# Sums taken from counts, two accumulators for the adj product, and score rows broadcast by transfers

## The chip, the core and the metric

The kernel runs on one core of a Trainium2 chip. The core has a matrix engine (TensorE, PE in the profile; its weight loads appear as PEld), a vector engine (DVE), a scalar engine (ACT), GpSimd (POOL) and a sync engine (SP) that issues most transfers. Each engine takes its instructions in the order in which the program issues them. The metric is device time in microseconds (us): 2310.74 before, the median of three runs (2310.22 to 2312.15).

## The reference, cut to what matters

Two graph layers over N = 3327 nodes of 256 features, with a weighted adjacency `adj` (3327 x 3327). Each layer's input is a layer norm followed by a Relu.

Layer 0 has two steps. Each step builds an attention matrix and keeps, per row, the largest probabilities that add up to 0.9:

```python
logits = q @ k.T                      # (N, N); q, k from Xa
probs = softmax(logits)
keep_sorted = cs - sp < TOP_P         # cs: running sum of sorted probabilities
A = probs * mask; A = A / A.sum(-1)
Xf = R @ Xf                           # R: adj plus identity, rows normalised
Xa = A @ Xa
Z = Z + Xf @ U1[n].T + Xa @ U2[n].T
```

After it come a residual, a layer norm and a second residual. Layer 1 is a four-head neighbour attention:

```python
e = leaky_relu(s[:, :, None] + d[:, None, :], 0.2)
attn = softmax(where(adj > 0, e, -inf), axis=2)
out = elu(einsum('hij,jhf->ihf', attn, hp))
```

## The kernel before, in words

The 3327 nodes are cut into NT = 26 row tiles of P = 128. All work is in `fast`; a second, long form, `general`, runs only if a test at the end of `fast` finds that a row's search failed.

**Order of the work.** The kernel doesn't write its instructions in a loop. Pieces of work are handed to a planner (`Plan.put`), each with its engine, an estimated length, a rank, the pieces it needs and the buffers it takes and gives back (for instance `accf`, `acca`, `px`, `pl`, `et`, `e`, `at`). The planner plays the pieces through with these estimates and issues them in the order that results. On the chip the order on each engine is then fixed.

**A row tile in a step of layer 0** (`search`, `attention`). PE makes the logits (L842), ACT takes their exponentials into a buffer `e` of 128 x 3327 and their sums (L853). A first threshold `t0` is guessed. Then the threshold is refined: the step needs, for the threshold t, how many elements of a row lie below it and what they add up to. Before the change both come from two passes of ACT over the row (`count`, L890): a Sign pass whose sum gives the count, and a Relu pass whose sum gives the sum below. POOL computes the next threshold from them (`step`, L905 to L932). Step 1 of the layer evaluates two thresholds (`EVALS`), so four ACT passes; step 2 evaluates three, the third with a pass of DVE instead (`sum_below`, L936). DVE then lists the candidates near the threshold (`window`, L947 and L952), picks the exact one (`sort`, `choose`) and zeroes the dropped elements in four pieces (`drop`, L1002). PE turns the row's 26 blocks of 128 x 128 (L1015, into `px`), ACT copies them to `et` (L1020, three buffers), and PE multiplies them with the features (L1027, into `acca`).

**The adj product** (`class Full`, `full`). For each row tile, 26 matmuls (L1053) add adj tiles times features into one PSUM accumulator, `accf`; adj comes through four buffers `at` of four tiles each (L1047). ACT copies the finished sum to `f` (L1060), DVE adds it up (L1069). There is one `accf`, so the next row tile's first matmul needs the copy of the last one. These products are PE's reserve: the planner puts them where softmax rows aren't ready.

**Layer 1's weights** (`layer1_weights`). One piece issues four loads (L706 to L709) into `late` and an `et` buffer and at once the DVE products and sums that need them (L713, L719), in another `et` buffer. It stands at the start of step 1, after the last use of the weights that lie in the same memory.

**From layer 0 to layer 1** (`finish2`). Each finished row is normed and projected (L1282, L1291); ACT copies the result and takes exponentials `qd` and `low` (L1296, L1297); DVE keeps the scores in `sd` (L1301).

**Layer 1** (`attend_neighbours`). The output nodes are cut into four blocks of W = 832. For a block, the exponentials of its source scores must stand on all 128 partitions (`both`): `broadcast` has PE transpose a column spread over 128 columns (L1460, four heads for each of seven tiles, into `px`), and ACT takes the exponential (L1464). The target is the memory of `c`, free only when all adj products are done. For each of the 26 neighbour tiles: two adj loads (L1500, 512-byte pieces), a mask on ACT (L1510 Relu, L1511 Sign, into `et`), four DVE operations, one per head (L1522), into one of six buffers (four `e`, two in the memory of `rhs`), then 8 product matmuls (L1538) and 8 matmuls for the sums (L1552, into the PSUM of `acca` and `accf`, three tiles at a time). At a block's end ACT copies the sums out (L1592, L1595), PE turns them (L1613), DVE and ACT finish (L1617, L1625 to L1630).

The functions that the change touches:

Of the kernel before, what the change touches and what calls it, by code (L numbers as in the profile page):

```python
# [19 lines left out]
P = 128  # L20
# [550 lines left out]
def fast(  # L571
# [35 lines left out]
    low = const.tile([P, NT, H], F32, name="low")  # L607

# [17 lines left out]
    with ExitStack() as l0:  # L626
# [73 lines left out]
        def layer1_weights():  # L700
# [8 lines left out]
            nc.sync.dma_start(wa[:, :, : H * FH], gat_w.rearrange("(c p) o -> p c o", p=P))  # L709
            prod = etpool.tile([P, 2, H, FH], F32, name="et")  # L710
# [9 lines left out]
            return g_all, b_all, wa  # L720
# [90 lines left out]
        plan = Plan(dict(pl=2, px=2, acca=1, accf=1, et=3, at=4, y=1, e2=2, mask=2, **BUFS))  # L811

        class Row:
# [3 lines left out]
                "b v w t0 t1 t2 u g k2 p0 p1 p2 p3 j0 j1 j2 j3 r0 s0 B0 B1 B2 q d dt least up h0 h1 room K zs nxt cnt m "  # L817
# [67 lines left out]
            def count(self, k, fn):  # L885

                junk = scr.tile([P, NP], mybir.dt.float8e5, name="junk")
                dst = (self.r0, self.s0)[fn == AF.Sign]
                t = (self.t0, self.t1, self.t2)[k]
                S.activation(junk[:, :N], self.e[:, :N], fn, bias=t, scale=-1.0, accum_out=dst, saturate=False)  # L890

            def step(self, k, eng):

# [10 lines left out]
                if k < 2:  # L904
                    TS(self.q, self.s0, float(N), t, ALU.add, ALU.mult)  # L905
                    TS(B, self.r0, -2.0, self.q, ALU.mult, ALU.add)
                else:
                    TS(B, B, 2.0, None, ALU.mult)
                TS(self.d, B, -0.5, self.b, ALU.mult, ALU.add)
                if k == 0:  # L910

                    TS(self.g, self.u, cs[:, self.i : self.i + 1], 0.25, ALU.mult, ALU.min)
                    TS(self.least, self.s0, N - 2.0 * (WIN[self.n] - 2), BIG, ALU.is_ge, ALU.mult)
                    TS(self.least, self.d, 0.0, self.least, ALU.is_ge, ALU.mult)
                else:
                    TT(self.u, B, (self.B0, self.B1)[k - 1], ALU.subtract)
# [16 lines left out]

            def sum_below(self):
                y = scr.tile([P, NP], BF16, name="y")
                V.scalar_tensor_tensor(  # L936
                    y[:, :N], self.e[:, :N], self.t2, self.e[:, :N], ALU.is_lt, ALU.mult, accum_out=self.B2
                )
# [98 lines left out]
        class Full:  # L1037


            def __init__(self, n, t):  # L1040
                self.n, self.t, self.at = n, t, {}
                self.src, self.w = (main, D + 1) if n == 0 else (c, D)

# [5 lines left out]
            def some(self, js):  # L1049
                for j in js:  # L1050
                    if j == 0:
                        self.acc = ps_a.tile([P, D + 1], F32, name="accf")
                    T.matmul(  # L1053
# [190 lines left out]
        def finish2(row, done, z, rank):  # L1244
# [48 lines left out]
            def stage():  # L1293
# [3 lines left out]
                S.activation(low[:, t, :], f[:, H * FH + H :], AF.Exp, scale=ALPHA - 1.0)  # L1297

# [22 lines left out]
            a = plan.put("ACT", 0.72, r, stage, needs=[a], take=["f"], give=["px", "xt"])  # L1321
            return plan.put("DVE", 0.6, r, scale, needs=[a], give=["f"]), s_
# [20 lines left out]
        def search(row, rank, keys, stats_of, fresh):  # L1343
# [22 lines left out]
            for j in range(2):  # L1366
                got = [plan.put("ACT", 3.05, rank - (2.1, 1.7)[j], row.count, j, fn, needs=[a]) for fn in (AF.Relu, AF.Sign)]
                a = plan.put("POOL", (3.8, 4.7)[j], rank - (2.0, 1.6)[j], row.step, j, GP, needs=[got, more])
            if EVALS[n] == 3:
                a = plan.put("DVE", 3.65, rank - 1.3, row.sum_below, needs=[a], take=["y"], give=["y"], lag=0.02, hold=3.6)  # L1370
# [36 lines left out]
        def full(n, t, rank, right, after):  # L1407
# [7 lines left out]
            for j in range(0, NT, 2):  # L1415
# [3 lines left out]
                    take=["accf"] * (j == 0), give=["at"] * last,  # L1419
                )  # L1420
            a = plan.put("ACT", 0.3, -90.0, f.copy, needs=[a], take=["f"], give=["accf"])
# [5 lines left out]
        def attend_neighbours(rows, ends, done, fulls):  # L1427
# [5 lines left out]
            logits_done = rows[-1].pieces["logits"]  # L1433
# [7 lines left out]
            def open_heads():  # L1441
                extra["both"] = halves_of("c", None)

            def open_more():
                extra["e"] = halves_of("rhs", None)

            opened = plan.put("SP", 0.02, 59.0, open_heads, needs=[fulls], lag=0.0)
            more = plan.put("SP", 0.02, 59.0, open_more, needs=[freed], lag=0.0)

            def broadcast(b, rank):  # L1450

                lo, hi = b * W, (b + 1) * W
                got = []
                for t in range(lo // P, -(-hi // P)):
                    held = {}

                    def turn(t=t, held=held):
                        held["pb"] = ps_x.tile([P, H, P], F32, name="px")
                        for k in range(H):
                            T.transpose(held["pb"][:, k, :], sd[:, 0, t, k : k + 1].to_broadcast([P, P]), ident)  # L1460

                    def exps(t=t, held=held):
                        x0, x1 = max(lo, t * P), min(hi, t * P + P)
                        S.activation(  # L1464
                            extra["both"][b % 2][:, :, x0 - lo : x1 - lo],
                            held["pb"][:, :, x0 - t * P : x1 - t * P],
                            AF.Exp,
                            scale=1.0 - ALPHA,
                        )

                    a = plan.put("PE", 0.55, rank, turn, needs=[ends[t][0], opened, used_heads[b % 2]], take=["px"])
                    got.append(plan.put("ACT", 0.65, rank, exps, needs=[a], give=["px"]))
# [5 lines left out]
            for b in range(4):  # L1478
# [14 lines left out]
                for j in range(NT):  # L1493
                    rank = r0 + 9.0 * j / NT
                    held = {}

                    def load(g, j=j, held=held, tiles=tiles):
# [15 lines left out]
                    def exponents(a, j=j, held=held, b=b):  # L1513
                        if a == 0:
                            k = j % 6
# [250 lines left out]
```

## Time and profile before

| engine | busy us | share of the span | what it mostly does |
|---|---|---|---|
| PE | 2223.0 | 96% | attention L1027 (623.6), adj product L1053 (322.8 and 317.0), layer-1 products L1538 |
| DVE | 1699.8 | 74% | window L947, L952, drop L1002, layer-1 exponents L1522 |
| ACT | 1559.9 | 68% | counts L890 (638.9, 208 of 3.07), copies L1020, exponentials L853 |
| POOL | 1017.6 | 44% | threshold steps L905 to L932 |

The span of the profiled run is 2307.9 us. The stages, from the windows of the trace: the start up to about 120 us; step 1 up to about 980; step 2 to about 1740; the passage to layer 1 to about 1820; layer 1 to about 2280; the end. A PE matmul of fp32 appears as two records, a transpose as one. The records' modelled ends overlap, so a busy PE is not necessarily a PE at its pace: the number of records in a window tells more. A line such as "PE px L1015 <- ACT et L1020" reads: this group of PE sat idle until that ACT group released it.

### The profile page before, as it was taken

What the parts mean: (1) busy time and instruction counts of PE and PEld (TensorE: products, weight loads), DVE (VectorE), ACT (ScalarE), POOL (GpSimd) and SP (SyncE); (2) the same over time, 40 slices, a digit from 0 to 9 for tenths busy, and PEclk for the clock granted to TensorE, in tenths of its full rate; (3) what the DMA queues carried; (4) which work ended last, traced back from release to release, by engine and by line L of the source; (5) the groups of instructions that cost most, each with busy time, mean ns of one, the idle gap of its engine ahead of it and who ended that gap; (6) DMA issues with size and microseconds to landing.
All of it is one profiled execution on the core that took longest, in us unless ns stands there. A gap on an engine that the chain in (4) does not pass through costs nothing. (4 is left out here: it accounts for less than half of the span.)

```text
span 2307.9 us, 36154 instructions
## 1 busy us (share of the span) xinstructions
PE 2223.0 (96%) x11956; PEld 1551.9 (67%) x11956; DVE 1699.8 (74%) x4299; ACT 1559.9 (68%) x2901; POOL 1017.6 (44%) x2263
## 2 busy tenths in 40 slices
PE   7989999999999999999999999999998999999997
PEld 5467777777877778777777778777877434333332
DVE  5564666656645664389889889889888797989895
ACT  5767788678777862488676787777773556565553
POOL 6345455445554541357766765677774000000000
PEclk9999999999999999999999999999999999999998
DMA  3021212212212222522212222122223343434341
GB/s 97 1 68 52 68 54 60 64 53 61 73 47 72 68 87 73 176 85 65 65 51 68 68 76 67 53 62 68 71 67 99 90 114 109 116 99 127 100 130 42
DMA packets 189654, 176.97 MB, mean 77 GB/s; under 512 B 14866, under 2 KB 145808, under 8 KB 189328
## 3 DMA queue, kind: packets, MB, share of 16 engines
q1 hardware_dynamic: 187472, 173.30, 25.8%
q8 instruction: 96, 1.57, 0.3%
q10 hardware_dynamic: 1984, 1.26, 0.2%
q14 instruction: 102, 0.84, 0.1%
HBM read 157.66 MB, written 15.89 MB: 75 GB/s over the span
## 5 line engine op out<-in xcount | busy, mean ns | idle before, releaser
L890 ACT ACTIVATE junk<-e,sc 128x3327 fp8e5<-128x3327 f32 x208 | 638.9, 3072 | 25.4 <-POOL sc L931 23.4
L1027 PE MATMUL acca<-rhs,et 128*128 128x256 f32 x2704 | 623.6, 381 | 2.3 <-ACT et L1020 2.2
L1027 PEld LDWEIGHTS acca<-rhs,et 128*128 128x128 f32 x2704 | 500.6, 191 | 66.9 <-ACT et L1020 4.8
L1053 PE MATMUL accf<-c,at 128*128 128x256 f32 x1352 | 322.8, 388 | 20.4 <-ACT f L1060 20.3
L947 DVE SCALAR_TENSOR_TENSOR y<-e,sc 128x1664 f32<-128x1664 f32 x104 | 204.6, 1967 | 187.0 <-POOL sc L928 169.3
L1053 PE MATMUL accf<-main,at 128*128 128x257 f32 x1352 | 317.0, 383 | 4.8 <-DMA at<-in_adjt_dram 4.5
L1020 ACT COPY et<-px 128x512 f32<-128x512 f32 (+1 forms) x364 | 194.4, 554 | 186.4 <-PE acca L1027 125.3
L1053 PEld LDWEIGHTS accf<-c,at 128*128 128x128 f32 x1352 | 251.6, 192 | 78.4 <-ACT f L1060 28.8
L1522 DVE SCALAR_TENSOR_TENSOR e<-c,low,et 128x832 f32<-128x832 f32 x288 | 289.1, 1075 | 16.8 <-ACT e L1592 9.5
L1053 PEld LDWEIGHTS accf<-main,at 128*128 128x128 f32 x1352 | 250.9, 191 | 46.4 <-issue 8.0
L952 DVE MAX8 cands<-y 128x8 f32<-128x208 f32 x832 | 241.1, 361 | 3.6
L1002 DVE SCALAR_TENSOR_TENSOR e<-e,thr 128x832 f32<-128x832 f32 x208 | 214.0, 1083 | 2.6 <-ACT kq L1178 0.5
L1538 PE MATMUL pl<-e,main 128*64 128x416 f32 x1152 | 212.6, 516 | 0.1
L1015 PE MATMUL px<-ident,e 128*128 128x128 f32 x1352 | 196.4, 277 | 16.8 <-ACT et L1020 7.9
L853 ACT ACTIVATE e<-pl 128x1024 f32<-128x1024 f32 x208 | 179.3, 865 | 45.6 <-PE pl L842 44.7
L1015 PEld LDWEIGHTS px<-ident,e 128*128 128x128 f32 x1352 | 163.4, 143 | 57.5 <-issue 13.6
L1511 ACT ACTIVATE et<-at 128x512 bf16<-128x512 f32 (+1 forms) x208 | 114.5, 550 | 118.3 <-DVE e L1522 76.9
L842 PE MATMUL pl<-kt,qq 64*128 64x512 f32 (+1 forms) x728 | 184.1, 588 | 0.0
L905 POOL TENSOR_SCALAR sc<-sc 128x1 f32<-128x1 f32 x104 | 40.2, 386 | 309.3 <-ACT junk L890 249.3
L1538 PEld LDWEIGHTS pl<-e,main 128*64 128x64 f32 x1152 | 79.6, 137 | 123.1 <-issue 104.0
L936 DVE SCALAR_TENSOR_TENSOR y<-e,sc 128x3327 bf16<-128x3327 f32 x26 | 95.5, 3672 | 47.9 <-POOL sc L931 47.9
L1522 DVE SCALAR_TENSOR_TENSOR rhs<-c,low,et 128x832 f32<-128x832 f32 x128 | 129.2, 1073 | 0.0
(485 smaller groups left out, 3076.8 us busy)
## 6 DMA issues: line engine op xcount, KB each, us to landing
at<-in_adjt_dram SPq DMA_DIRECT2D x416, 256.0 KB, 2.8
at<-in_adjt_dram SPq DMA_DIRECT2D x104, 192.0 KB, 3.0
at<-in_adjt_dram SPq DMA_DIRECT2D x52, 128.0 KB, 2.1
ys<-ystage SPq DMA_DIRECT2D x26, 256.0 KB, 2.4
rhs<-in_x_dram SPq DMA_DIRECT2D x26, 128.0 KB, 3.3
ystage<-in_x_dram SPq DMA_DIRECT2D x26, 128.0 KB, 2.1
base<-ys SPq DMA_DIRECT2D x26, 128.0 KB, 2.2
x1s<-ystage SPq DMA_DIRECT2D x26, 128.0 KB, 1.7
```

Source lines behind the costliest of these rows:

```text
L842: T.matmul(pl[:, r, :m], qq[half, self.i, :], kt[half, 512 * k : 512 * k + m], start=True, stop=True,)
L853: S.activation(self.e[:, 1024 * k : 1024 * k + pl.shape[1]], pl, AF.Exp, accum_out=(self.p0, self.p1, self.p2, self.p3)[k],)
L890: S.activation(junk[:, :N], self.e[:, :N], fn, bias=t, scale=-1.0, accum_out=dst, saturate=False)
L947: V.scalar_tensor_tensor(self.y[:, : hi - lo], self.e[:, lo:hi], self.up, self.e[:, lo:hi], ALU.is_lt, ALU.mult, accum_out=(self.h0, self. ...
L952: V.max(self.cands[:, o // PIECE, :], self.y[:, o - lo : min(o + PIECE, hi) - lo])
L1002: V.scalar_tensor_tensor(piece, piece, self.thr[:, o : o + 1], piece, ALU.is_gt, ALU.mult)
L1015: T.transpose(pt[:, k, :], self.e[:, j * P : (j + 1) * P], ident)
L1020: S.copy(self.et[g][:, :m, :], self.pt.pop(g)[:, :m, :])
L1027: T.matmul(self.acc, et[:, j - 4 * g, :], rhs[self.n][:, j, :], start=(j == 0), stop=(j == NT - 1))
L1053: T.matmul(self.acc[:, : self.w], self.at[j // JC][:, j % JC, :], self.src[:, j, : self.w], start=(j == 0), stop=(j == NT - 1),)
L1522: V.scalar_tensor_tensor(held["e"][:, k, :], extra["both"][b % 2][:, k, :], low[:, j, k : k + 1], held["mask"], ALU.max, ALU.mult,)
L1538: T.matmul(q["acc"][a][k * FH : (k + 1) * FH, c, :C], main[:, j, h * FH : (h + 1) * FH], held["e"][:, h, c * C : (c + 1) * C], start=(j == 0),
```

## The change

Four things, in one edit.

1. **Sums from counts.** The sum below the first threshold is still measured (a Relu and a Sign pass). For each later threshold only the Sign pass runs, and the sum is the previous sum plus the number of elements between the two thresholds times the mean of the two. Step 1 has three ACT passes per row in place of four; step 2 has four as before, the third threshold's now on ACT, and `sum_below` on DVE is gone.
2. **Two adj accumulators in step 2.** `accf` becomes 128 x 2 x 256 there, and row tiles take its halves in turn.
3. **Layer 1's weights in two pieces**: the loads, once the fourth row of step 1 is done, and the DVE work as a piece of its own.
4. **Score rows by transfers.** ACT takes the exponential of a row tile's source scores where the scores are made (`high`), SP stores it to memory on the device as `highs` (4 x 3328), and a block's rows come back with two broadcasting transfers. Block 0's target is the memory of `qq`, free once the last logits are done; its first two neighbour tiles have buffers of their own for adj (the memory of `kt`) and for the mask (that of the counts' output); a third `e2` buffer makes seven. The transposes L1460 and the exponentials L1464 go.

The core of the diff:

```diff
-                dst = (self.r0, self.s0)[fn == AF.Sign]
+                dst = (self.s0, self.s1, self.s2)[k] if fn == AF.Sign else self.r0
...
-                if k < 2:
-                    TS(self.q, self.s0, float(N), t, ALU.add, ALU.mult)
+                s = (self.s0, self.s1, self.s2)
+                if k == 0:
+                    TS(self.q, s[0], float(N), t, ALU.add, ALU.mult)
                     TS(B, self.r0, -2.0, self.q, ALU.mult, ALU.add)
                 else:
-                    TS(B, B, 2.0, None, ALU.mult)
+                    TS(self.q, t, (self.t0, self.t1)[k - 1], 0.5, ALU.add, ALU.mult)
+                    TS(self.u, s[k], s[k - 1], self.q, ALU.subtract, ALU.mult)
+                    TT(B, (self.B0, self.B1)[k - 1], self.u, ALU.add)
...
-                got = [plan.put("ACT", 3.05, rank - (2.1, 1.7)[j], row.count, j, fn, needs=[a]) for fn in (AF.Relu, AF.Sign)]
+                got = [
+                    plan.put("ACT", 3.05, rank - (2.1, 1.7)[j], row.count, j, fn, needs=[a])
+                    for fn in (AF.Relu, AF.Sign)[j:]
+                ]
...
-                a = plan.put("DVE", 3.65, rank - 1.3, row.sum_below, needs=[a], take=["y"], give=["y"], lag=0.02, hold=3.6)
+                a = row.pieces["counted"] = plan.put("ACT", 3.05, rank - 1.4, row.count, 2, AF.Sign, needs=[a])
...
-                    if j == 0:
+                    if j == 0 and self.n == 0:
                         self.acc = ps_a.tile([P, D + 1], F32, name="accf")
+                    elif j == 0:
+                        if self.t == 0:
+                            late["accf"] = ps_a.tile([P, 2, D], F32, name="accf")
+                        self.acc = late["accf"][:, self.t % 2, :]
...
-                layer1_ready = plan.put("DVE", 3.0, base + NT - 1.0, layer1, needs=[used], lag=3.0)
+                a = plan.put("SP", 0.5, base + 4.0, layer1, needs=[used, done[3]], take=["et"], lag=8.0)
+                layer1_ready = plan.put(
+                    "DVE", 3.7, base + 5.0, lambda: layer1_scores(late["wa"], late["a"]), needs=[a], take=["et"],
+                    give=["et", "et"],
+                )
...
+                S.activation(high[:, t, :], f[:, H * FH : H * FH + H], AF.Exp, scale=1.0 - ALPHA)
+            def spread():
+                nc.sync.dma_start(highs[:, t * P : (t + 1) * P].rearrange("h p -> p h"), high[:, t, :])
...
-                        for k in range(H):
-                            T.transpose(held["pb"][:, k, :], sd[:, 0, t, k : k + 1].to_broadcast([P, P]), ident)
+                    def fetch(a=a):
+                        nc.sync.dma_start(
+                            extra["both"][b % 2][:, 2 * a : 2 * a + 2, :],
+                            highs[2 * a : 2 * a + 2, lo:hi].partition_broadcast(P),
+                        )
...
+                    if b == 0 and j < 2:
+                        loads, own = plan.put("SP", 0.2, rank, load_first, needs=[opened[0]], lag=4.0), []
+                        m_ = plan.put("ACT", 1.8, rank, mask_first, needs=[loads])
```

## The prediction

> **What bounds the kernel now.** I read the page's busy table first, then twenty-microsecond windows, then the waits of TensorE (PE), then the timeline wherever a window showed PE short of work.
>
> ```profile
> PE 2223.0 (96%) x11956; PEld 1551.9 (67%) x11956; DVE 1699.8 (74%) x4299; ACT 1559.9 (68%) x2901; POOL 1017.6 (44%) x2263
> ...
> PEclk9999999999999999999999999999999999999998
> ```
>
> PE is busy 96% of the span at full clock, so time is saved only by taking work off PE or by filling its pauses. The windows say where the pauses lie (columns: PE, PEld, DVE, ACT, POOL busy, granted clock, DMA share, GB/s):
>
> ```profile
> 120.00:140.00 20.00, 13.33 (x60) 10.92 (x59) 13.28 (x35) 8.08 (x17) 5.46 (x18) 0.83 0.28 91
> ...
> 700.00:720.00 20.00, 20.00 (x102) 14.83 (x101) 6.25 (x16) 13.71 (x20) 12.04 (x29) 1.00 0.22 70
> ...
> 1460.00:1480.00 20.00, 14.87 (x63) 12.48 (x63) 17.76 (x50) 16.58 (x24) 11.72 (x26) 0.83 0.30 85
> ...
> 1780.00:1800.00 20.00, 17.57 (x80) 14.14 (x80) 5.75 (x21) 5.35 (x12) 1.90 (x5) 0.88 0.09 27
> ...
> 1940.00:1960.00 20.00, 20.00 (x130) 8.41 (x131) 19.83 (x30) 17.86 (x52) 0.00 (x0) 1.00 0.53 156
> ```
>
> Step 1 (to about 980 us) leaves nothing once it runs; its start, step 2 (980 to 1740), the passage to layer 1 (1740 to 1820) and the block boundaries of layer 1 do. The waits of PE name one cause above all:
>
> ```profile
> PE accf L1053 <- ACT f L1060: 20.6, 18, 5.1
> PE px L1015 <- ACT et L1020: 7.9, 6, 5.3
> ```
>
> The 18 waits (20.6 us) are the adj product of the next row tile waiting until ScalarE (ACT) has copied the last one out of `accf`; ACT gets to that copy only after the 3.07 us counts in its queue. 19.6 of the 20.6 lie between 900 and 1700 us. The longest of the second row is at the start of step 1, where this chain ends:
>
> ```profile
> 126.67 0.43 DVE L713 TENSOR_TENSOR et<-late,et 128x256 f32<-128x256 f32 x1 [5.74 <-DMA late<-in_gat_w_dram]
> ...
> 129.87 1.09 ACT L1020 COPY et<-px 128x512 f32<-128x512 f32 x2 [5.39 <-DVE et L713]
> ...
> 130.50 1.11 PE L1015 MATMUL px<-ident,e 128*128 128x128 f32 x4 [5.32 <-ACT et L1020]
> ...
> 131.41 3.62 PE L1027 MATMUL acca<-rhs,et 128*128 128x256 f32 x8
> ```
>
> VectorE (DVE) waits for layer 1's weights while it holds two of the three `et` buffers. And the passage:
>
> ```profile
> 1774.52 1.04 PE L1460 MATMUL px<-ident,sd 128*128 128x128 f32 x8
> ...
> 1779.75 2.91 PE L1015 MATMUL px<-ident,e 128*128 128x128 f32 x12 [4.20 <-ACT c L1464]
> ...
> 1804.37 3.12 PE L1460 MATMUL px<-ident,sd 128*128 128x128 f32 x20 [0.20 <-ACT c L1464]
> ...
> 1805.65 15.99 DVE L1522 SCALAR_TENSOR_TENSOR e<-c,low,et 128x832 f32<-128x832 f32 x16
> ```
>
> The score broadcasts hold the two `px` buffers while the last row wants them, and DVE, done with that row at 1781, starts layer 1 only at 1805.65.
>
> **What the Trainium skill says.** "Perfetto Trace Analysis", Identifying the Most-Contended Engine, calls matmul busy share a poor measure because pipelined matmuls look smaller; the trace agrees: 1940 to 1960 reads 20.00 of 20 busy with 130 matmuls, where the windows around it hold 140 to 160. So I also count by pace. Its Optimizing Tensor Performance, Matmuls, wants independent groups in different PSUM banks so that evacuation overlaps; the 20.6 us are what one accumulator costs. "PSUM — Partial Sum Buffer", PSUM bank collisions, says that two engines in one bank are not stalled (an error is raised instead): both new halves share a bank, so I charge no time; no trace here shows it. "DMA: Bandwidth & Descriptors", Specifications, puts pieces under 512 B at a read-modify-write; before has no 4-byte pieces.
>
> **The change part by part.**
>
> *Counts.* In step 1 each row loses one Relu count, 26 x 3.07 = 80 us of ACT; PE there is full, so this buys nothing. In step 2 each row swaps its second Relu count for a Sign count at the third threshold and drops the DVE sum (L936, 26 of 3.68 us = 96 us). ACT stays level, DVE falls from 664 busy of 760 us (87%) to 568 (75%), and POOL keeps the same number of small operations per row. The row's chain loses one 3.07 us count. This is slack, not path, while PE is the bound: I price it at zero, but it makes the next part safe.
>
> *Two accumulators.* The first adj matmul of a row tile now waits for no copy of the tile just before it. Up to the 20.6 us go, with one or two more for clock: after the 5.1 us wait of window 1460 the clock is 0.83. Other waits (rows not ready, adj tiles not landed) will take part of it. 22 at most, 6 at least, I take 15.
>
> *Layer 1's weights loaded after row 3 and summed later.* Saves 5.3 of waiting, 0.7 before it, and the slow restart: eight matmul records in 3.62 where the pace is 1.73, and about 0.8 in the lines around. That is 8.5. Two of three `et` buffers are still held for some 4 us, now among other work: 0 to 4 back. I take 7 (4 to 8.5).
>
> *Broadcast by transfer, first half.* 112 transposes go (L1460). Eight take 1.04, so 0.13 each: 14.6 us of PE, and 28 exponentials of about 0.6 on ACT. Fifty-six of them, blocks 0 and 1, stand in the passage: 7.3 us.
>
> *The passage itself.* From 1753.74 to 1823.58 PE spent 69.8 us. Its work at pace: 52 attention matmuls of 0.432 (eight records in 1.73) = 22.5; 40 transposes = 5.2; 16 adj matmuls = 6.9; two rows' projections at 1.4 = 2.8; broadcasts 7.3; three tiles of products and sums at 4.29 (48 records and the sums recur every 12.86) = 12.9. Sum 57.6, so 12.3 us were waits. In the order of the changed program 34 adj matmuls stand before the last row's attention and 14 after it, and products follow at once; tiles 0 and 1 have masks and score rows in buffers of their own, so DVE can make them right after the last row's drop. Tile 2's mask comes after the last `f` copy (0.4 + 2.2 on ACT, 2 on DVE: 4.6 us), within the 5.7 us that PE spends on tiles 0 and 1. I take 9 of 12.3 (4 to 12.3); with the transposes 16 (11 to 19.6).
>
> *Block boundaries.* Like points of blocks 1, 2 and 3 (1958.14, 2079.44, 2199.78) are 121.3 and 120.3 apart. Work: 26 tiles of 4.29 = 111.5, 21 output transposes 2.7, broadcasts 3.6, sum 117.8: 3 us lost per boundary, because DVE first stands idle for buffers and then lags:
>
> ```profile
> 1924.22 4.07 DVE L1522 SCALAR_TENSOR_TENSOR e<-c,low,et 128x832 f32<-128x832 f32 x4 [5.33 <-PE accf L1552]
> ...
> 1943.84 2.28 PE L1538 MATMUL pl<-rhs,main 128*64 128x416 f32 x8
> ```
>
> Eight records in 2.28 where 1.43 is the pace. A seventh buffer (`e2` 3) lets DVE do 4 us more in its idle time. The other 56 transposes give 7.3 outright, the boundaries 5 of 9 (0 to 9): 12 (7.3 to 16.3).
>
> *What is added.* An exponential of 128x4 per row (0.2 on ACT, beside L1296 at 0.21), hidden. A scatter of 512 pieces of 4 B per row on SyncE's queue: as many pieces as a layer-1 adj load of 256 KB has, at 512 B each, which lands in 3.0 us; doubled for the read-modify-write, an estimate of 6. Nothing needs it soon. But its issue waits for ACT, with adj loads queued behind it; four `at` buffers hold 4 x 4 x 0.432 = 6.9 us of PE work. Two transfers of 852 KB per block (128 partitions x 2 x 832 x 4 B): between 3.0 (256 KB) and 9.4 us (`qq<-qqs`, 1472 KB), and from block 2 on half a block ahead of need. I price these at zero; the bound is the last rival.
>
> Sum: 15 + 7 + 16 + 12 = 50 us. 2310.7 - 50 = 2261; ends 28 (2282) and 66 (2244).
>
> **Rivals.** (a) Step 2 gives its part back: PE, no longer held by `accf`, reaches the transposes before the drops are done. For: PE waits 2.9 us on DVE there already. Against: DVE gains 3.7 us per row. Saving 35, 2276. (b) DVE becomes the bound of layer 1: per block 104 operations of 1.0 (16 in 15.99) plus seven outputs of 1.0 = 111 against 114.2 on PE, a margin of 3 us. Then the boundaries lose what the transposes gave and the passage gives 11: 7 + 15 + 11 + 0 = 33, 2278. (c) Slower: SyncE's queue. If each scatter delayed the adj loads until PE stood 2.5 us, 26 x 2.5 = 65 against 50 gives 2326. Against: in step 2 before, which already has waiting stores in that queue, PE never waited for an adj load. A row leaving its window (24 or 32 wide) would run the long fallback; worked through on these inputs the rows keep at most 22 and 25, so I give that nothing.
>
> **How the numbers follow.** Forecast 0.62, (a) 0.17, (b) 0.14, (c) 0.07. Predicted 2261. The range takes in (a) and (b) with some room, 2246 to 2286, and leaves out (c) and the far ends. Faster 0.92, same 0.02, slower 0.06.
>
> **What would show it.** Right: no wait of `accf` on `f` in step 2; window 120 to 140 full; no L1460 transposes, and DVE's first layer-1 operation within 5 us of the last drop; blocks 115 to 118 us apart. Wrong: PE waits on `at` loads or on drops in step 2, or products that wait for DVE at the start of each block.

## The result and the profile after

The changed kernel takes 2345.67 us (median of four runs, 2340.18 to 2351.34) beside 2310.6 for the kernel before: ratio 1.0151, interval 1.0126 to 1.0176. It is slower by 35 us; 2261 was forecast.

First the page of the changed kernel, the table of busy time (the engines in the order of the line shown before):

```profile
PE 2228.7 (95%) x11844; PEld 1552.8 (66%) x11844; DVE 1619.9 (69%) x4273; ACT 1470.7 (63%) x2843; POOL 925.6 (39%) x2263
```

PE has 112 records fewer, the transposes that went, and is nevertheless busy 5.7 us longer. ACT and DVE lost about what they were meant to lose (89 and 80 us), and POOL 92 us with as many instructions as before. So the work went away, and something else came. The windows of the changed kernel say where (same columns as before):

```profile
120.00:140.00 20.00, 20.00 (x114) 16.46 (x113) 18.01 (x59) 15.31 (x28) 10.48 (x19) 1.00 0.01 1
700.00:720.00 20.00, 20.00 (x99) 16.01 (x97) 10.69 (x38) 14.48 (x28) 7.68 (x23) 1.00 0.09 26
1080.00:1100.00 20.00, 15.43 (x62) 12.57 (x63) 12.30 (x39) 12.11 (x22) 11.94 (x28) 0.83 0.46 126
...
1600.00:1620.00 20.00, 17.50 (x84) 14.10 (x85) 5.53 (x12) 12.61 (x17) 8.86 (x29) 0.85 0.32 88
1780.00:1800.00 20.00, 17.86 (x86) 15.38 (x87) 10.51 (x29) 8.32 (x13) 5.42 (x16) 0.83 0.67 204
```

The hole at 120 to 140 us is filled, as forecast. But windows of step 2 and of the passage (1780 us) now have holes, with the clock down to 0.83 in them. A table by stage, each boundary read from the first or last start of a group of matmuls (first adj product of step 2, last logits, first and last layer-1 product); "pieces of 16 bytes" is the first experiment:

| us | step 1 | step 2 | passage | layer 1 | end | span |
|---|---|---|---|---|---|---|
| before | 972.8 | 731.2 | 103.4 | 474.8 | 25.7 | 2307.9 |
| after | 959.8 | 776.0 | 110.3 | 477.4 | 26.0 | 2349.5 |
| pieces of 16 bytes | 958.4 | 713.1 | 89.4 | 470.9 | 25.7 | 2257.5 |

Step 1 is 13 us shorter. Step 2 is 45 us longer and the passage 7. The list of PE's waits in the changed kernel has a new head, and the old one is almost gone:

```profile
PE accf L1062 <- DMA at<-in_adjt_dram: 63.4, 18, 5.8
...
PE accf L1062 <- ACT f L1069: 2.9, 7, 0.5
```

Before, the first of these was 4.5 us in one wait and the second 20.6 in 18. One instance, in the timeline of the sync queue and then of PE (start, length, group):

```profile
1071.67 0.38 SPq L1310 DMA_DIRECT2D highs<-high  x1
1074.67 14.40 SPq L1051 DMA_DIRECT2D at<-in_adjt_dram  x5
```

```profile
1072.65 6.31 PE L1062 MATMUL accf<-c,at 128*128 128x256 f32 x28
1084.11 2.07 PE L1062 MATMUL accf<-c,at 128*128 128x256 f32 x4 [5.15 <-DMA at<-in_adjt_dram]
1086.64 9.09 PE L1062 MATMUL accf<-c,at 128*128 128x256 f32 x32 [0.46 <-ACT f L1069]
```

The scatter of a score row is issued at 1071.67; the adj loads follow from 1074.67 on. PE works off the tiles that it has and then stands 5.15 us for the next. Its first four records after that take 2.07 us where four take 1.03 elsewhere: the wait is paid again as a slow restart. The Trainium skill, "TensorE: Matmul & The Clock Gate", What's actually happening, says that a stretch of some 3.4 us without work halves PE's clock and that about as long a stretch of work brings it back. The trace agrees, with a longer slow stretch at this place: a mean of 0.83 over 20 us is 6.8 us at half clock (0.17 x 20 / 0.5).

How long the transfers take, from issue to landing: the scatters on the page of transfers, then the adj loads of step 2 (1000 to 1740 us; least, median, most):

```profile
base<-ys SPq DMA_DIRECT2D x26, 128.0 KB, 7.2
...
highs<-high SPq DMA_DIRECT2D x26, 2.0 KB, 9.8
```

```profile
DMA to landing us min/median/max: 2.0/6.6/11.6
```

Two kilobytes take 9.8 us. The adj loads' median is 6.6 us; before it was 2.7 in the same stretch. The loads of `base`, 7.2 us here, took 2.2 before. At the start of layer 1 the last scatter (1844.43) stands just ahead of the fourth neighbour tile's loads (1845.31), and ACT's timeline shows the mask waiting for them:

```profile
1857.85 0.63 ACT L1543 ACTIVATE at<-at 128x512 f32<-128x512 f32 x1 [9.24 <-DMA at<-in_adjt_dram]
```

### The profile page after: what moved, and what is told of

Read it like the earlier page. It is cut to its first block, busy times and chain, and to the rows that moved or that the text cites. A ratio compares the mean times of both kernels' runs of the same rounds, so it can differ in the third digit from the quotient of the medians.

```text
span 2349.5 us, 35943 instructions
## 1 busy us (share of the span) xinstructions
PE 2228.7 (95%) x11844; PEld 1552.8 (66%) x11844; DVE 1619.9 (69%) x4273; ACT 1470.7 (63%) x2843; POOL 925.6 (39%) x2263
## 5 line engine op out<-in xcount | busy, mean ns | idle before, releaser
L895 ACT ACTIVATE junk<-e,sc 128x3327 fp8e5<-128x3327 f32 x182 | 559.1, 3072 | 59.5 <-POOL sc L940 58.0
L1062 PE MATMUL accf<-c,at 128*128 128x256 f32 x1352 | 339.0, 402 | 61.5 <-DMA at<-in_adjt_dram 58.9
L1062 PEld LDWEIGHTS accf<-c,at 128*128 128x128 f32 x1352 | 263.2, 201 | 120.7 <-DMA at<-in_adjt_dram 55.5
L1544 ACT ACTIVATE et<-at 128x448 bf16<-128x448 f32 (+1 forms) x204 | 112.2, 550 | 132.5 <-DVE e L1555 78.3
L1571 PE MATMUL pl<-e,main 128*64 128x416 f32 x1024 | 189.2, 519 | 2.3 <-DVE e L1555 2.2
L1571 PEld LDWEIGHTS pl<-e,main 128*64 128x64 f32 x1024 | 72.1, 138 | 112.0 <-issue 91.6
L1555 DVE SCALAR_TENSOR_TENSOR e<-c,low,et 128x832 f32<-128x832 f32 x128 | 128.6, 1073 | 4.2 <-PE accf L1585 2.1
L1543 ACT ACTIVATE at<-at 128x448 f32<-128x448 f32 (+1 forms) x204 | 109.9, 539 | 31.4 <-DMA at<-in_adjt_dram 31.0
L1555 DVE SCALAR_TENSOR_TENSOR e<-qq,low,et 128x832 f32<-128x832 f32 x120 | 120.6, 1076 | 12.3 <-ACT et L1544 9.3
L847 PEld LDWEIGHTS pl<-kt,qq 64*128 64x128 f32 x728 | 70.9, 185 | 82.2 <-issue 77.2
```

What stands on the lines that cost most here:

```text
L847: T.matmul(pl[:, r, :m], qq[half, self.i, :], kt[half, 512 * k : 512 * k + m], start=True, stop=True,)
L1062: T.matmul(self.acc[:, : self.w], self.at[j // JC][:, j % JC, :], self.src[:, j, : self.w], start=(j == 0), stop=(j == NT - 1),)
L1555: V.scalar_tensor_tensor(held["e"][:, k, :], extra["both"][b % 2][:, k, :], low[:, j, k : k + 1], held["mask"], ALU.max, ALU.mult,)
L1571: T.matmul(q["acc"][a][k * FH : (k + 1) * FH, c, :C], main[:, j, h * FH : (h + 1) * FH], held["e"][:, h, c * C : (c + 1) * C], start=(j == 0),
```

## The experiments

Three theories at first. **A**: the scatter's small pieces hold the transfer engines up, and adj loads behind them land late. **B**: the sync queue stands before each scatter until ACT has made the row (its list of waits has 49.3 us of that), so the loads behind are issued late. **C**: it isn't the scatter; step 2 suffers from the third count's new place on ACT. Unless said otherwise an edit is made to the changed kernel. Every edit that changes a piece's length, buffers or engine may also change the planner's order; the first one leaves every order as it is. The number behind each result is its ratio to the kernel before, with the 95% interval.

**1. Pieces of 16 bytes.** The row goes out node by node, not head by head. It is read back as before, so the factors come back permuted: the kernel does the same work on other numbers.

```diff
-                nc.sync.dma_start(highs[:, t * P : (t + 1) * P].rearrange("h p -> p h"), high[:, t, :])
+                rows = highs.rearrange("h n -> (h n)")[t * P * H : (t + 1) * P * H]
+                nc.sync.dma_start(rows.rearrange("(p h) -> p h", h=H), high[:, t, :])
```

> The changed kernel, but each score row goes out as 128 pieces of 16 bytes, one behind the other in memory, in place of 512 pieces of 4 bytes; the order of every engine and queue is the same. It permutes the high factors, so the output is another. Theory A (the small pieces hold the DMA engines for some 8 us, and the adjacency loads behind them in the queue land late: 63 us of PE waiting): with a quarter of the pieces the scatter lands in 3 to 4.5 us, loads behind it in 3 to 5 us, which the tiles loaded ahead cover; PE waits on adjacency loads under 10 us, time 2270 to 2290. Theory B (the queue stands before the scatter until ScalarE has made the row: 49 us of such waits): the queue's order is unchanged, so PE's waits stay near 60 us and the time within 2335 to 2350. Theory C (the search chain with its third count on ScalarE is what slows step 2): also unchanged, 2335 to 2350.

Measured: 2259.59 us, ratio 0.9782 (0.9766 to 0.9799). The transfers of this kernel, its waits of PE, and its sync queue's waits:

```profile
highs<-high SPq DMA_DIRECT2D x26, 2.0 KB, 1.9
```

```profile
PE accf L1062 <- ACT f L1069: 4.5, 8, 1.2
PE accf L1062 <- DMA at<-in_adjt_dram: 4.2, 1, 4.2
```

```profile
SPq L1311 <- ACT high L1307: 49.8, 15, 8.1
```

It is the scatter, as theory A says; B and C fall: with every order unchanged and the queue standing 49.8 us as before, the scatter lands in 1.9 us, and 59 us of PE's waits are gone. Theory A's sizes were missed: the landing was to be 3 to 4.5 us, and the time is 10 us under its range. The account of the 92.0 us between the two spans (2349.5 and 2257.5): waits for adj loads 63.4 - 4.2 = 59.2; busy time of PE for the same 11844 records 2228.7 - 2197.9 = 30.8. The mean clocks, 0.979 and 0.993, give that alone: 2197.9 x 0.993 / 0.979 = 2229.3. Together 90.0. So a third of the damage is the clock.

**2. The small pieces on ACT's own queue.**

```diff
                 S.activation(high[:, t, :], f[:, H * FH : H * FH + H], AF.Exp, scale=1.0 - ALPHA)
+                nc.scalar.dma_start(highs[:, t * P : (t + 1) * P].rearrange("h p -> p h"), high[:, t, :])
```

> The changed kernel with the same 512 pieces of 4 bytes, but issued from ScalarE's queue right behind the Exp that makes them; the sync queue holds nothing in their place. Theory A1 (pieces delay only what stands behind them in their own queue): the adjacency loads land in 2.8 us again, PE waits under 10 us, 2270 to 2290. Theory A2 (pieces occupy the DMA engines for every queue): the loads still land in 5 to 9 us while a scatter is under way and the time is 2310 to 2345. Theory B (the queue stands until ScalarE is done): as A1, 2270 to 2290. Theory C: 2335 to 2350.

Measured: 2360.01 us, ratio 1.0206 (1.0187 to 1.0225). Its transfers and waits:

```profile
highs<-high ACTq DMA_DIRECT2D x26, 2.0 KB, 10.4
```

```profile
PE accf L1062 <- DMA at<-in_adjt_dram: 68.8, 22, 5.6
```

A2: another queue doesn't help, and the time lies 15 us above A2's range. The Trainium skill, "DMA: Bandwidth & Descriptors", Issuing engines are not separate DMA queues, says that transfers of all issuing engines run on the same 16 transfer engines and mix there. The trace agrees as far as it goes: loads on SP's queue are late beside a store on ACT's. Memory shared by the two queues would give the same.

**3. The rows turned by PE**, two more matmuls for each row tile, stored as 4 pieces of 512 bytes.

```diff
+                for k in range(2):
+                    T.matmul(held["ph"], late["wa"][:, k, H * FH : H * FH + H], held["xt"][:, k, :], start=(k == 0), stop=(k == 1))
...
-                S.activation(high[:, t, :], f[:, H * FH : H * FH + H], AF.Exp, scale=1.0 - ALPHA)
+                S.activation(high[:, 0, :], held["ph"], AF.Exp, scale=1.0 - ALPHA)
```

> The changed kernel, with the four score columns of a row of nodes computed a second time as four rows of 128 by two more matmuls per row of nodes (4 x 128 out), the Exp taken on those, and stored as 4 pieces of 512 bytes. The output is the reference's. Theory A: the store lands in about 2 us, loads in 2.8; PE waits on adjacency loads under 6 us; 52 matmuls more at 0.25 to 0.3 us add 13 to 16 us at most (beside 14.6 us of removed transposes): 2265 to 2285. Theory B: 2335 to 2360, for the store still waits for ScalarE at the same place. Theory C: 2340 to 2365.

Measured: 2272.85 us, 0.9840 (0.9823 to 0.9856); adj loads cost one wait of 4.7 us. Theory A again. The added matmuls account for the 13.3 us above experiment 1: 104 records, and four of them take 0.60 with 0.53 to the next group: 26 x 0.53 = 13.8.

**4. No transfers: the old broadcast by PE**, the other edits kept (the diff puts `turn` and `exps` of the kernel before back and takes `high`, `spread` and `fetch` out).

> The changed kernel without its transfers: the score rows of the last layer are broadcast by PE transposes and ScalarE copies as in the kernel before; the counts, the two accumulators, the split loads and the two neighbour tiles in buffers of their own stay. By the prediction's terms (step 2 -15, layer-1 weights -7, and perhaps half of the passage's -9) 2280 to 2290; the waits on the accumulator's copy are gone. Theories A and B: there is no scatter, so PE waits on adjacency loads under 6 us: 2275 to 2295. Theory C: step 2 is as long as in the changed kernel, 2330 to 2350.

Measured: 2271.69 us, 0.9833 (0.9817 to 0.9849), lower than the terms of the prediction give. Stages (step 1, step 2, passage, layer 1) 960.9, 707.3, 104.7, 474.1. It also says what the transfers bring when they cost nothing: 2271.69 - 2259.59 = 12.1 us.

**5. The scatter by itself**: the kernel before with only this.

```diff
+                S.activation(high[:, t, :], f[:, H * FH : H * FH + H], AF.Exp, scale=1.0 - ALPHA)
+            def spread():
+                nc.sync.dma_start(highs[:, t * P : (t + 1) * P].rearrange("h p -> p h"), high[:, t, :])
...
+            plan.put("SP", 0.1, r, spread, needs=[a], lag=4.0)
```

> The kernel before with nothing added but the high Exp and the 26 scatters of 512 pieces of 4 bytes; what they store is not read. Theory A (the pieces hold up the adjacency loads): PE waits on adjacency loads rise from 4.5 to 45 to 70 us and the time goes to 2350 to 2375. Rival D (the kernel before has slack in its loads, and the scatter hurts only together with the changed kernel's other edits): under 2325. The waits on the accumulator's copy, 20.6 us, stay or are partly covered by the new ones.

Measured: 2361.79 us, 1.0233 (1.0216 to 1.0250), 53.6 us for something that nobody reads. Adj waits 28.9 us, another 4.7 booked to a count on ACT, and a mean clock of 0.978: less waiting than expected, the same loss. Rival D falls: the scatter needs none of the other edits to do harm.

The other parts of the change, each alone on the kernel before:

**6. Two accumulators.** The hunks of `class Full` and of its pieces in the plan.

```diff
-                    take=["accf"] * (j == 0), give=["at"] * last,
+                    take=[f.bank] * (j == 0) + ["accf"] * (n == 1 and t + j == 0), give=["at"] * last,
```

> The kernel before with the second accumulator alone. The prediction's term is -15 us, between -6 and -22: 2288 to 2304, with the waits on the accumulator's copy in step 2 down from 19.6 to under 4 us. Rival a of the prediction (PE then waits on the drops instead): 2304 to 2311 with waits on DVE's kept scores in their place.

Measured: 2301.5 us, 0.9971 (0.9959 to 0.9984): -6.7 and not -15. Its waits of PE:

```profile
PE px L1015 <- ACT et L1020: 16.9, 15, 4.8
PE accf L1059 <- ACT f L1066: 8.4, 18, 0.9
```

The accumulator's waits fell by 12.2 us, but those for ACT's copies of the turned blocks rose by 9.0 (from 7.9); the rise lies in the passage. A wait took the place of the one removed, though not the one that the expectation named.

And 8.2 us of the accumulator's waits stay in step 2, where under 4 were expected. The place shown above, 1072 to 1087 us of the changed kernel, shows how. ACT's copy of the accumulator there reads:

```profile
1086.22 0.37 ACT L1069 COPY f<-accf 128x256 f32<-128x256 f32 x1 [6.89 <-PE accf L1062]
```

The row tile that it copies was finished at 1077.2 us (its 52nd record). Yet the copy begins only when PE has ended twelve records of the next tile, which go into the other half; and then PE waits 0.46 us for the copy. Experiment 6 has the same: in none of the 26 copies of step 2 does an adj record begin while the copy runs, and 18 times the next one begins 0.05 us after its end. So the halves work as one buffer: a copy waits for the matmuls put ahead of it, whichever half they write, and those behind wait for the copy. The second half only lets the next tile's first records, mostly four, pass ahead. Whether the hardware or the order that the program sets among the users of one buffer asks for this, no run shows.

**7. Layer 1's loads split** (`layer1_loads`, `layer1_scores` and their two pieces).

> The kernel before with the split of layer 1's loads alone. The prediction's term is -7 us (-4 to -8.5): 2299 to 2305, with the 5.3 us wait of PE on ScalarE's copy at 130 us gone. Rival: the wait only moves, 2306 to 2312.

Measured: 2301.07 us, 0.9962 (0.9950 to 0.9975): -9.0, in step 1 (972.8 to 962.8). The 5.3 us wait is gone: PE's waits for `et` copies fell from 7.9 us in 6 to 1.9 in 4.

**8. The counts alone** (`count`, `step`, `sum_below` and their pieces).

> The kernel before with the counts alone changed. The prediction's term is nothing (slack, not path): 2306 to 2313, VectorE's busy time in step 2 down by some 95 us with PE's idle time unchanged. Rival: the search is on the path in step 2, and freeing VectorE of 26 times 3.7 us lets the accumulator's copy or the drops come sooner: 2290 to 2303. Theory C (the third count on ScalarE is worse placed): over 2316.

Measured: 2275.16 us, 0.9852 (0.9835 to 0.9868): -33 us from the part that I had priced at nothing, below every range written down for it. By stage, step 1 took 962.1 and step 2 709.3: 10.7 and 21.9 us less than before. Its wait on the accumulator's copy, with one accumulator still:

```profile
PE accf L1051 <- ACT f L1058: 6.0, 10, 1.9
```

Before, this was 20.6. In 960 to 1700 us it fell from 19.4 to 3.4, PE's busy time rose from 717.3 to 731.6, and its records from 3511 to 3619. What stands in the way, the timeline of ACT before shows at the longest of these waits:

```profile
1466.00 3.07 ACT L890 ACTIVATE junk<-e,sc 128x3327 fp8e5<-128x3327 f32 x1
...
1469.19 3.07 ACT L890 ACTIVATE junk<-e,sc 128x3327 fp8e5<-128x3327 f32 x1
...
1472.26 0.35 ACT L1060 COPY f<-accf 128x256 f32<-128x256 f32 x1
...
1472.66 2.07 PE L1053 MATMUL accf<-c,at 128*128 128x256 f32 x4 [5.13 <-ACT f L1060]
```

Two counts of a pair stand in ACT's queue ahead of a copy of 0.35 us, and PE waits for the copy. With sums from counts only the first threshold has a pair.

**9. The four heads of a node side by side**, in memory and in the broadcast tiles.

```diff
-                                extra["both"][b % 2][:, k, :],
+                                extra["both"][b % 2][:, :, k],
```

> The changed kernel with the high factors kept node by node, the four heads of a node side by side, in memory and in the broadcast tiles: the score row goes out as 128 pieces of 16 bytes, the broadcasts read whole runs, and VectorE reads one head with a step of 16 bytes. The output is the reference's. Theory A: as with the pieces of 16 bytes, 2256 to 2266, if VectorE's operation keeps its 1.07 us. Rival E: the stepped read costs VectorE over 8 percent an operation, so that a block of layer 1 (109 us of VectorE in 117) is bound by it: 2275 to 2330. Theory B (the queue stands for ScalarE): 2335 to 2350.

Measured: 2497.09 us, 1.0818 (1.0799 to 1.0836). Rival E, 167 us beyond its range. The stores are harmless (they land in 2.4 us), but DVE's line in layer 1 now reads:

```profile
L1555 DVE SCALAR_TENSOR_TENSOR e<-qq,low,et 128x832 f32<-128x832 f32 x120 | 199.5, 1747 | 0.0
```

1747 ns in place of 1076, for one operand with a step of 16 bytes. Layer 1 takes 706.8 us. The Trainium skill, "SBUF — State Buffer", Door 1: The DMA port swizzle, has a remark that full rate needs at least two accesses to each 16-byte line; a step of 16 bytes has one, and the trace agrees. The remark goes on that one can stride "for free" by 4 fp32, which can be read as this very step; so read it is wrong here.

**10. Groups of rows turned at once**: one transpose for six or seven row tiles.

```diff
+                src = high[:, first_t : t + 1, :].rearrange("p t h -> p (t h)")
+                T.transpose(held["ph"][: src.shape[1], :], src, ident)
...
+                for i in range(first_t, t + 1):
+                    nc.sync.dma_start(highs[:, i * P : (i + 1) * P], turned[(i - first_t) * H : (i - first_t + 1) * H, :])
```

> The changed kernel, but the high factors of six or seven rows of nodes are turned together by one PE transpose (four in all), copied by ScalarE, and stored as 24 or 28 pieces of 512 bytes; the output is the reference's. Theory A: no small pieces are left, four transposes cost some 0.3 us of PE each, the rest is the kernel with pieces of 16 bytes (2259.6): 2256 to 2266. Theory B (any store that waits for ScalarE on the sync queue costs): four such waits are left of 26, 2265 to 2290.

Measured: 2260.8 us, 0.9790 (0.9774 to 0.9806): faster than both kernels, with the whole computation kept. The page of this kernel:

```profile
PE 2195.4 (97%) x11848; PEld 1533.8 (68%) x11848; DVE 1619.5 (72%) x4273; ACT 1468.6 (65%) x2847; POOL 931.9 (41%) x2263
```

Four records more than the changed kernel, 33 us less of PE time: nearly all of that is the clock (at the changed kernel's mean clock 2195.4 would be 2195.4 x 0.993 / 0.979 = 2226.8).

**11. Counts and two accumulators** together on the kernel before.

> The kernel before with the counts and the two accumulators, nothing else. If the two take away the same waits (the accumulator's copy behind counts on ScalarE), little is left for the second: 2270 to 2276, beside 2275.2 for the counts alone. If they add up, 2275.2 - 6.7 = 2268.5 or less, down to 2260 with the -15 of the prediction.

Measured: 2275.71 us, 0.9853 (0.9837 to 0.9870), the same as the counts alone. Both take away the same wait; the second finds nothing.

**12. Counts, with the third threshold's sum left on DVE** (`sum_below` stays; only the second evaluation loses its Relu pass).

> The kernel before with the new formula for the second evaluation alone: ScalarE loses its second Relu count (52 of 3.07 us over both steps), VectorE keeps its sum of the third evaluation (26 of 3.68 us). If the counts' gain of 33 us comes from ScalarE's relief (its copies stand behind fewer counts), 2262 to 2282. If it comes from VectorE's relief in step 2, only step 1's share is left: 2294 to 2306. If from neither but from the order that the planner then chooses, it may lie anywhere, and waits on the accumulator's copy would tell.

Measured: 2271.11 us, 0.9830 (0.9814 to 0.9847). The 96 us of `sum_below` on DVE stay, and so does the gain (39.0 us, beside 33.0): it goes with ACT's relief, not with DVE's. POOL, 91 us less busy in experiment 8, is back at 1021.9 us here, so it isn't POOL's either.

Two pairs on what makes the scatter slow. All are the kernel before with stores that nobody reads, as in experiment 5.

**13 and 14. Fewer pieces of 4 bytes; as many pieces of 16.**

```diff
+                nc.sync.dma_start(highs[0:1, t * P : (t + 1) * P].rearrange("h p -> p h"), high[:, t, 0:1])
```

> The kernel before with 26 scatters of one head alone: 128 pieces of 4 bytes each, which nothing reads (the run with 512 pieces of 4 bytes took 2361.8 us, and its scatters landed in some 10 us). If the number of pieces is what costs: landing in 2 to 4 us, time 2306 to 2320. If a piece of 4 bytes is dear in itself however few they are: landing in 5 us or more, time 2320 to 2345.

```diff
+                nc.sync.dma_start(highs[:, t * P : (t + 1) * P, :].rearrange("c p h -> p c h"), high[:, t : t + 1, :].to_broadcast([P, 4, H]))
```

> The kernel before with 26 stores of 512 pieces of 16 bytes each (every row four times over), which nothing reads. If the number of pieces is what costs, it is as with 512 pieces of 4 bytes: landing in 8 to 11 us, time 2345 to 2370. If the size of 4 bytes is what costs, landing in 2 to 4 us, time 2306 to 2325.

Measured: 2335.94 us, 1.0111 (1.0095 to 1.0128), and 2306.32 us, 0.9988 (0.9981 to 0.9995). Landing, first the 128 pieces of 4 bytes, then the 512 of 16:

```profile
highs<-high SPq DMA_DIRECT2D x26, 0.5 KB, 8.3
```

```profile
highs<-high SPq DMA_DIRECT2D x26, 8.0 KB, 3.3
```

It isn't the count. Half a kilobyte in 128 pieces is nearly as slow as four times that in 512.

**15 and 16. The same 128 pieces, 512 or 64 bytes apart** (`highs` of 3328 x 128 or x 16, its first column written).

```diff
+                nc.sync.dma_start(highs[t * P : (t + 1) * P, 0:1], high[:, t, 0:1])
```

> The kernel before with 26 stores of 128 pieces of 4 bytes, as in the run that took 2335.9 us, but each piece 512 bytes from the next in memory instead of side by side; nothing reads them. If neighbouring small pieces are written one after another, because they change the same stretch of memory (128 in some 8 us, 65 ns each), these land in 2 to 3 us and the time is 2304 to 2314. If a write of 4 bytes is dear in itself, they land in 7 to 9 us again, 2325 to 2345.

> The same with 64 bytes from piece to piece. If the stretch in which writes go one after another is 64 bytes or less, as the run 512 bytes apart: landing 2 to 3 us, 2304 to 2314. If it is larger (up to 512 bytes, so that 8 pieces share one), landing in between, 2.5 to 5 us. If a write of 4 bytes is dear in itself: 7 to 9 us, 2325 to 2345.

Measured: 2308.24 us, 0.9989 (0.9983 to 0.9996), and 2307.7 us, 0.9986 (0.9979 to 0.9993). The pieces 512 and then 64 bytes apart:

```profile
highs<-high SPq DMA_DIRECT2D x26, 0.5 KB, 1.4
```

```profile
highs<-high SPq DMA_DIRECT2D x26, 0.5 KB, 1.6
```

Neither the count nor the size of 4 bytes alone is dear. Pieces of 4 bytes are slow where they lie side by side. That they are written one after another would fit: 128 neighbours of one head in 8.3 us would be 65 ns each, and four heads, each a run of its own, take 9.8 to 10.2 and not four times 8.3. That order inside the memory was not seen itself.

The packets in the traces say where the time is not lost. In experiments 13 and 15 alike, the slow store and the quick one, a store's own packets take about 9 ns each and are mostly over within 0.2 us of the first; in the changed kernel, within 0.4. What stretches are the packets behind them: in the 10 us after one store (1082 to 1092 us of experiment 13, 1083 to 1093 of experiment 15) 0.33 MB took 71% of the transfer engines' time, and 0.85 MB took 33%. So theory A has to be put otherwise: it isn't the small pieces that keep the transfer engines busy, but the loads behind them. They seem to be held up past the engines, where no trace looks.

## Why the prediction was wrong

**The step that failed: "What is added".** "I price these at zero; the bound is the last rival." Measured: 86.1 us (2345.67 - 2259.59; 2260.8 in experiment 10, with nothing permuted, says the same). Three parts of that step were off.
- The landing. I took the pieces of a load of the same number, doubled for the read-modify-write: 6 us. It was 9.8, and for a reason that counts of pieces don't hold: the pieces are neighbours. The 6.9 us of work in four `at` buffers would just have covered 6.
- The mechanism that I feared, "its issue waits for ACT, with adj loads queued behind it", was there (49.3 us) and cost nothing that shows (experiment 1 has it too).
- My evidence against rival (c) was that the queue of the kernel before has waiting stores and PE never waits for an adj load. Those stores go in long runs and land in about 2 us (`x1s<-ystage` 1.7). They said nothing on pieces of 4 bytes.

Rival (c) was the outcome, at a chance of 0.07. Its waiting was well sized in total (26 x 2.5 = 65 us, against 63.4), though by luck: it came in 18 waits, not 26. Its time was not: 2326, because it left out the slow restarts, 30.8 us of clock. I had seen a clock of 0.83 after one wait before, and charged it there, but not here.

**The other terms.** Without the scatter's cost the forecast of 2261 is met, 2259.6, and that is largely luck. By stage the gain was 14.4, 18.1, 14.0 and 3.9 us (step 1, step 2, passage, layer 1), where 7, 15, 16 and 12 had been forecast: errors of both signs cancel.
- Counts: priced at zero, worth 33, of which 10.7 in step 1, where "this buys nothing". "This is slack, not path" looked at DVE's share. The path was in the list of waits, which I had quoted: a copy behind counts. I named the counts as its cause and then gave the whole gain to the accumulator.
- Two accumulators: 15 forecast, 6.7 alone, nothing beside the counts (2275.71 and 2275.16). That a row tile's first matmul "waits for no copy of the tile just before it" holds for its first records only. The prediction charged no time for two halves in one bank; 8.2 us of waiting are there, whatever asks for them.
- Weights: 7 forecast, 9.0 alone. Right (its upper end, 5.3 + 0.7 + 1.9 + 0.8, adds up to 8.7 and not to 8.5); but the counts too take most of it, step 1 being 962.1 with the counts, 962.8 with the split and 960.9 in experiment 4 with both. The three edits, the first tiles' own buffers and the seventh buffer are together worth 2309.57 - 2271.69 = 37.9, only some 5 us more than the counts alone.
- Passage: 16 forecast, 14.0 measured between the kernel before and experiment 1. From experiment 4, which has the first tiles' own buffers, to experiment 1 it is 15.3; the buffers alone didn't shorten it (103.4 and 104.7). So it is the transposes and their wait on ACT that went.
- Boundaries: 12 forecast, 3.9 in all of layer 1, below the range of 7.3 to 16.3: not even the 7.3 that the transposes were to give outright came. At the prediction's like points the blocks were 121.3 and 120.3 us apart; in experiment 1 it is 118.9 both times, still 4.7 more than a block's work at pace without broadcasts (111.5 + 2.7 = 114.2), where 3 was the loss charged before. So the seventh buffer shows no gain. At the start of a block PE still follows DVE: eight products take 2.61 us there (at 2020.82 in experiment 1), where 1.43 is the pace.

Rival (a) didn't come: in experiment 1 PE waits for drops 2.2 us in all, 2.9 before. Rival (b) came in part: DVE is not the bound of layer 1 (busy 110 of the 118.9 us), but the boundaries took back about half of what the transposes were to give.

**Signs.** Most of what I listed for "right" came true in the changed kernel: window 120 to 140 full, no transposes, the first layer-1 operation on DVE within a microsecond of the last drop at 1825.2. Two signs came nearly: the waits on `f` were to be none and are 2.9 us in all, and the blocks were to be 115 to 118 us apart and are 118.9. The first sign of "wrong" came in full, PE's waits on `at` loads in step 2, and the last in small, products that wait for DVE (2.3 us on `rhs`). None of the signs for "right" touches the scatter.

What stays open: how much of the counts' 33 us is the shorter queue of ACT itself and how much the new order in which the planner then lays the work; what orders copies and products of the two halves; what past the transfer engines makes neighbouring small writes slow; and from which distance on they are quick, between 4 and 64 bytes.

## What to carry to other kernels

A transfer is priced by how long it takes to land and by the loads under way with it, whichever queue issued them, and not by its bytes: 2 KB a row cost 86 us here. Turn data so that a store goes out in runs (here four transposes for 26 rows) instead of storing it element by element. A wait that two edits could remove is counted once, and a wait of several microseconds on PE is counted with the slow restart after it, here half as much again.

## What the hardware showed that I had not expected

- Stores of 4 bytes to neighbouring addresses: 8.3 us for 128, 9.8 for 512; 1.4 to 1.6 us when they lie 64 or 512 bytes apart; 1.9 for 128 neighbours of 16 bytes. The stores' own packets are over within 0.2 to 0.4 us in the slow and the quick case.
- While such a store of 512 pieces is under way, adj loads land in 7.0 to 9.4 us (1072 to 1082 us of the changed kernel) in place of 2.7, and in 7.3 to 9.7 when the store is on another queue.
- DVE reading one of its two fp32 tensor operands with a step of 16 bytes: 1747 ns in place of 1076.
